# Own orders for the first two periods and the seventh period of a four-stage pipeline on one Trainium2 core

## The chip, the cores and the metric

The kernel runs on 1 core of one Trainium2 chip. The metric is device time in microseconds (us) of one execution. Three runs of the kernel before gave 4455.59, 4456.53 and 4457.14 us; the median is 4456.53 us.

## The reference

The input is `x`, four sequences of 2048 rows of 256 channels (float32). Four blocks follow each other, each wrapped as `x = x + layernorm(block(layernorm(x)))`:

```python
x = x + LN(softmax_attention(LN(x)))      # 16 heads of 16, q and k are scaled copies of the input, v is the input
x = x + LN(channel_mix(LN(x)))            # xk, xr: mixes of a row with the row before it; r = sigmoid(xr Wr)
                                          # out = r * (relu(xk Wk)^2 Wv)
x = x + LN(linear_attention_layer(LN(x))) # own LN, q/k through elu+1, message = Q (K^T V) / normaliser, residual,
                                          # own LN, gelu MLP 256 -> 1024 -> 256, residual
x = x + LN(gated_mlp(LN(x)))              # weights int32 / 127; silu(gate) * up, 256 -> 768 -> 256
```

The linear attention sums `K^T V` over all 2048 rows of a sequence, so the message of any row can only be made once the whole sequence has passed its keys and values.

## The kernel before, in words

The softmax attention comes first and is not touched. The rest of the reference is in `rest`. It cuts the 4 x 2048 rows into 16 blocks of 512 rows (`IB`, 4 blocks per sequence, `NBLK`), and gives each block four stages, written as Python generators that stop at named parts:

- `stage_f` is the channel mix. Parts: `sums` (statistics of the layernorm, on VectorE), `norm` (on ScalarE, after a power on GpSimd), `turn` (TensorE transposes into `hT`, ScalarE copies, and two VectorE copies that carry the last column to the next block), `mix` (ScalarE `shift`, VectorE `xk` and `xr`), `k0`, `k1`, `r`, `v` (matmuls), `osums`, `x` (output norm, residual on GpSimd, and a DMA that writes the block to the DRAM tile `mid`). Block 0 has no `sums` and `norm`: its `h0` is made ahead.
- `stage_a` is the first half of the linear attention: `sums`, `norm`, `norm2`, `turn`, `q0`, `q1` (into `QT`, through `elu1`), `kv0` to `kv4` (keys and values, gathered into one PSUM accumulator).
- `stage_b` is its second half: `pre`, `msg`, `sums`, `norm`, `turn`, `up0` to `up3`, `down0` to `down3`, `osums`, `x`.
- `stage_i` is the gated MLP: `sums`, `norm`, `turn`, `gate0` to `gate5`, `down0` to `down3`, `osums`, `x`.

A loop runs over 24 periods `p`. In period `p`, stage f is at block `p`, stage a at block `p-2` (`LAG_A`), stage b at block `p-6` (`LAG_B`), stage i at block `p-7` (`LAG_I`). So periods 0 and 1 hold stage f alone, periods 2 to 5 hold f and a, period 6 is the first with stage b, period 7 the first with stage i. `next:` and `last:` in an order name a part of the period after or before; parts of blocks outside 0 to 15 are skipped.

The order of the parts within a period is a written string: `RAMP` for periods 0 to 5, `FULL` for 6 to 17, `TURN` for 18, `LATE` after that. The instructions of TensorE (PE), ScalarE (ACT) and VectorE (DVE) go through `InOrder`, which keeps them in the program's order; they all carry line 46 in the profile. GpSimd (POOL) instructions and the DMAs issued by SyncE (SP) are placed by the scheduler. An engine works its own list strictly in order.

Resources that tie the parts: the pool `ps_m` has 5 PSUM tiles, taken in turn by every `mm_tile()`; `ps_t` has 2; the tag `tmp` (`shift`, `elu`, `gs`) has 3; `xk` and `r` share one buffer; `hT` has one. `convert` turns the int32 weights of the gated MLP into `wgT`, `wuT`, `wdT`: a DMA into a staging tile `wi`, then one DVE instruction. All three stagings use the one buffer of the tag `gT`. Before, `convert` runs at the start of periods 0, 1 and 2.

Of the kernel before, what the change touches and what calls it, by code (L numbers as in the profile page):

```python
# [49 lines left out]
def rest(ctx: ExitStack, tc: tile.TileContext, a: dict, out_rows, mids, env: dict, narrow: bool):  # L50
# [17 lines left out]
    NB = B * NBLK  # L68
    LAG_A, LAG_B, LAG_I = 2, 2 + NBLK, 3 + NBLK
# [11 lines left out]
    def convert(name):  # L81
        wi = one.tile(list(wq[name].shape), I32, tag="gT", name="wi")
        nc.sync.dma_start(out=wi, in_=a[name].rearrange("(c p) d -> p c d", p=P))
        dve.tensor_scalar(wq[name], wi, 1.0 if narrow else DEQUANT, None, ALU.mult)

    kvms, vs = [], []
    for r in range(3):
# [5 lines left out]
        v = one.tile([P, CC, P + 4], FP, tag=f"v{r}", name=f"v{r}")  # L93
# [57 lines left out]
    def load(j, pool):  # L151
        xs[j] = pool.tile([P, 4, C], FP, tag="x", name="x")
        nc.sync.dma_start(out=xs[j], in_=mids[j // NBLK][j % NBLK])
# [192 lines left out]
    def stage_i(j):  # L346
# [67 lines left out]
    FULL = (  # L414
        "f:turn i:turn b:msg i:gate0 a:turn f:mix last:i.osums i:gate1 b:sums last:i.x load i:gate2 "
        "i:gate3 f:k0 b:norm f:k1 f:r b:turn i:gate4 b:up0 i:gate5 f:v b:up1 f:osums b:up2 f:x b:up3 "
        "a:q0 next:f.sums b:down0 a:q1 next:a.sums b:down1 next:f.norm b:down2 next:a.norm b:down3 "
        "a:kv0 next:b.pre i:down0 b:osums a:kv1 i:down1 b:x a:kv2 next:a.norm2 i:down2 next:i.sums "
        "a:kv3 i:down3 a:kv4 next:i.norm"
    )  # L420
    RAMP = (
        "load f:turn a:turn f:mix a:q0 a:q1 f:k0 f:k1 next:a.sums a:kv0 a:kv1 next:a.norm a:kv2 "
        "next:f.sums a:kv3 f:r next:a.norm2 a:kv4 f:v next:f.norm f:osums f:x next:b.pre"
    )

    TURN = (
        "i:turn b:msg i:gate0 last:i.osums b:sums i:gate1 last:i.x load b:norm i:gate2 "
        "b:turn b:up0 next:b.pre b:up1 b:up2 b:up3 b:down0 b:down1 b:down2 b:down3 b:osums i:gate3 "
        "i:gate4 b:x i:gate5 next:b.msg i:down0 next:i.sums next:b.sums i:down1 "
        "next:i.norm i:down2 next:b.norm i:down3 next:i.turn"  # L430
    )
    LATE = (
        "last:i.osums b:turn b:up0 last:i.x load b:up1 b:up2 next:b.pre b:up3 b:down0 b:down1 b:down2 "
        "b:down3 b:osums i:gate0 i:gate1 b:x i:gate2 i:gate3 i:gate4 next:b.msg i:gate5 next:i.sums "
        "i:down0 next:b.sums i:down1 next:i.norm i:down2 next:b.norm i:down3 next:i.turn"
    )
    MAKE = {"f": (stage_f, 0), "a": (stage_a, LAG_A), "b": (stage_b, LAG_B), "i": (stage_i, LAG_I)}
    live = {}

    def step(p, stage, part):  # L440
        make, lag = MAKE[stage]
        j = p - lag
        if not 0 <= j < NB:
            return
        if (stage, j) not in live:
            live[stage, j] = make(j)
        name = next(live[stage, j])
        assert name == part, (stage, j, name, part)

    xs[0] = env["x0"]  # L450
    for p in range(NB + LAG_I + 1):
        if p < 3:
            convert(("wgT", "wuT", "wdT")[p])
        order = LATE if p > NB + LAG_A else TURN if p == NB + LAG_A else FULL if p >= LAG_B else RAMP
        for item in order.split():
            if item == "load":
                if p + 1 < NB:
                    load(p + 1, early)
                if 0 <= p + 1 - LAG_B < NB:
                    load(p + 1 - LAG_B, late)  # L460
                continue
            stage, part = item.split(":")
            at = p
            if stage in ("next", "last"):
                at = p + 1 if stage == "next" else p - 1
                stage, part = part.split(".")
            step(at, stage, part)
# [3 lines left out]
def sandwich_kernel(ctx: ExitStack, tc: tile.TileContext, a: dict, out: bass.AP):  # L471
# [490 lines left out]
    with tc.If(narrow == 1) as branch:  # L962
        rest(tc, a, out_rows, mids, env, True)
    with branch.Else():
        rest(tc, a, out_rows, mids, env, False)
# [54 lines left out]
```

## Time and profile before

| what | value |
|---|---|
| median of 3 runs | 4456.53 us |
| the profiled execution | 4454.68 us |
| its span, first to last instruction | 4452.8 us |
| PE busy over the span | 4186.2 us, 94% |
| DVE busy | 3380.2 us, 76% |
| ACT busy | 2853.3 us, 64% |
| POOL busy | 1098.8 us, 25% |
| mean granted PE clock | 0.98 |

`rest` begins at about 3030 us of the span. The busy times by period, with the boundaries put near the first `xk` matmul of a period (period 7 and 8: near the first gate matmul):

| stretch (us) | period | length | PE busy | DVE busy | ACT busy | POOL busy | PE clock |
|---|---|---|---|---|---|---|---|
| 3030 to 3064 | 0 | 34.00 | 16.73 | 17.70 | 14.65 | 11.12 | 0.70 |
| 3064 to 3091 | 1 | 27.00 | 20.84 | 17.48 | 13.00 | 15.89 | 0.84 |
| 3091 to 3125 | 2 | 34.00 | 28.62 | 21.51 | 19.95 | 15.23 | 0.95 |
| 3125 to 3159 | 3 | 34.00 | 28.71 | 22.02 | 20.53 | 10.42 | 0.95 |
| 3159 to 3193 | 4 | 34.00 | 28.51 | 21.50 | 19.76 | 10.43 | 0.95 |
| 3193 to 3229 | 5 | 36.00 | 26.44 | 25.84 | 20.52 | 12.70 | 0.91 |
| 3229 to 3299 | 6 | 70.00 | 61.34 | 35.11 | 29.32 | 26.48 | 0.90 |
| 3299 to 3377 | 7 | 78.00 | 73.82 | 37.98 | 46.28 | 30.32 | 1.00 |
| 3377 to 3459 | 8 | 82.00 | 75.88 | 42.63 | 46.28 | 39.54 | 0.98 |

How to read it: an average over the span says little here, as nearly 3030 us of it are the softmax attention. The change touches only periods 0, 1, 2 (its start) and 6. There no engine is full, so what counts is which engine waits for which, in order of time. Lines of the timeline give a start, a duration, the engine, the source line, the operation with `out<-in` by tile name, and in brackets the idle time before it and what ended that. A PE matmul on float32 shows as two instructions of the program's one.

### The profile page before, as it was taken

How to read it: one execution, taken by the hardware profiler on the slowest of the kernel's cores; microseconds unless marked ns; L12 is line 12 of the kernel's file. 1: busy time of each engine (PE TensorE's matmuls, PEld its weight loads, DVE VectorE, ACT ScalarE, POOL GpSimd, SP SyncE). 2: the span in 40 equal slices, each digit the busy share in tenths (PEclk: the TensorE clock that was granted, in tenths of full speed). 3: DMA queues.
4: the chain of work that ended last, by engine and by line, in shares of the span. 5: the costliest groups of instructions: out<-in, count | busy, mean ns of one | idle time of the engine just before them, and what ended most of it. 6: DMA issues, size and time to landing. Idle time of an engine off the chain costs nothing.

```text
span 4452.8 us, 69661 instructions
## 1 busy us (share of the span) xinstructions
PE 4186.2 (94%) x26369; PEld 2199.2 (49%) x26369; DVE 3380.2 (76%) x6734; ACT 2853.3 (64%) x3550; POOL 1098.8 (25%) x1655
## 2 busy tenths in 40 slices
PE   6999999999999999999999999986889899998998
PEld 3444444444444444444444444433456666666666
DVE  7888999988889998889998888865645545545333
ACT  2777777777777777777777777764555555554333
POOL 3011012310101321111131010003344444544344
PEclk9999999999999999999999999998999999999998
DMA  3001001110010110101011000002100000000000
GB/s 110 24 26 30 20 20 36 52 29 20 21 38 11 39 48 25 34 12 28 25 39 41 17 23 23 17 25 74 38 14 25 22 31 24 29 20 10 20 20 16
DMA packets 84570, 130.60 MB, mean 29 GB/s; under 512 B 21376, under 2 KB 41984, under 8 KB 84224
## 3 DMA queue, kind: packets, MB, share of 16 engines
q1 hardware_dynamic: 79184, 123.28, 9.2%
q8 instruction: 210, 3.44, 0.3%
q10 hardware_dynamic: 5040, 2.77, 0.2%
q14 instruction: 136, 1.11, 0.1%
HBM read 33.70 MB, written 25.17 MB: 13 GB/s over the span
## 4 chain that ended last, share of the span: by engine, by line
PE 72%; DVE 14%; ACT 8%; issue 3%; POOL 2%; DMA 1%; SPq 0%; ACTq 0%; DVEq 0%; POOLq 0%
PE acc L46 21%; PE s L46 19%; PE w L46 15%; PE m L46 14%; DVE mx L46 6%; PE t L46 2%; ACT h L46 1%; ACT p L46 1%; ACT L46 1%; DVE o L46 1%; DVE gs L46 1%; DVE lno_st L46 1%; ACT gs L46 1%; PE ot L46 1%; ACT zT L46 1%
## 5 line engine op out<-in xcount | busy, mean ns | idle before, releaser
L46 DVE TENSOR_REDUCE mx<-s 128x1 f32<-128x512 f32 x4096 | 2538.9, 683 | 249.8 <-PE s L46 249.6
L46 ACT ACTIVATE p<-w 128x1024 f32<-128x1024 f32 x2048 | 1995.7, 1022 | 808.6 <-PE s L46 515.5
L46 PE MATMUL s<-k,q 64*128 64x512 f32 x4096 | 1665.1, 450 | 29.9 <-DMA q<-lo 16.9
L46 PE MATMUL w<-mrow,pick 64*128 64x512 f32 x4096 | 1398.3, 417 | 0.0
L46 PE MATMUL w<-q,k 64*128 64x512 f32 x4096 | 1369.8, 419 | 0.0
L46 PEld LDWEIGHTS s<-k,q 64*128 64x128 f32 x4096 | 758.2, 186 | 1233.8 <-DVE mx L46 1123.2
L46 PE MATMUL acc<-p,xp 128*32 128x512 f32 x8192 | 1092.5, 605 | 0.0
L46 PEld LDWEIGHTS w<-mrow,pick 64*128 64x128 f32 x4096 | 748.8, 185 | 55.7
L46 PEld LDWEIGHTS w<-q,k 64*128 64x128 f32 x4096 | 669.9, 185 | 57.9 <-ACT p L46 21.0
L745 POOL TENSOR_SCALAR xm<-nm 128x16 fp32r<-128x16 f32 x64 | 17.6, 274 | 1565.9 <-DVE nm L46 1546.1
L46 PEld LDWEIGHTS acc<-p,xp 128*32 128x32 f32 x8192 | 161.6, 108 | 247.9 <-issue 246.7
L46 PE MATMUL m<-zT,w1T 128*128 128x512 f32 x512 | 229.5, 603 | 5.9 <-ACT zT L46 5.9
L46 PE MATMUL m<-w2T,hf 128*128 128x256 f32 x1024 | 225.6, 379 | 0.0
L46 PEld LDWEIGHTS m<-w2T,hf 128*128 128x128 f32 x1024 | 194.6, 190 | 38.4 <-issue 13.4
L46 DVE SCALAR_TENSOR_TENSOR gs<-m,gs 128x512 f32<-128x512 f32 x96 | 66.2, 690 | 193.5 <-ACT gs L46 159.1
L46 ACT ACT_TABLE_LOAD x94 | 120.6, 1283 | 117.2 <-PE m L46 83.2
L626 POOL TENSOR_SCALAR xp<-x,lnx_nm,lnx_rs 128x64 f32<-128x64 f32 x256 | 99.1, 394 | 374.5 <-PE acc L46 373.6
L644 POOL TENSOR_SCALAR xd<-x,lnx_nm,lnx_rs 128x128 f32<-128x128 f32 x256 | 110.8, 447 | 292.6 <-PE t L46 285.2
L46 ACT ACTIVATE elu<-elu 128x256 f32<-128x256 f32 (+1 forms) x96 | 46.8, 488 | 182.1 <-DVE elu L46 177.1
L46 PEld LDWEIGHTS m<-zT,w1T 128*128 128x128 f32 x512 | 97.5, 193 | 123.6 <-issue 98.4
L46 ACT ACTIVATE hf<-m,b 128x512 f32<-128x512 f32 x128 | 86.6, 686 | 99.3 <-PE m L46 98.8
L46 ACT CAST gT<-gs 128x512 fp32r<-128x512 f32 x96 | 59.4, 619 | 138.5 <-DVE gs L46 138.5
(160 smaller groups left out, 4265.0 us busy)
## 6 DMA issues: line engine op xcount, KB each, us to landing
q<-hi SPq DMA_DIRECT2D x256, 64.0 KB, 2.1
q<-lo SPq DMA_DIRECT2D x256, 64.0 KB, 2.1
mid<-x SPq DMA_DIRECT2D x31, 512.0 KB, 2.6
x<-mid SPq DMA_DIRECT2D x31, 512.0 KB, 3.3
k<-hi SPq DMA_DIRECT2D x240, 64.0 KB, 2.1
k<-lo SPq DMA_DIRECT2D x240, 64.0 KB, 2.1
x<-in_x SPq DMA_DIRECT2D x16, 512.0 KB, 5.6
out<-x SPq DMA_DIRECT2D x16, 512.0 KB, 2.8
```

Source lines behind the costliest of these rows:

```text
L46: return lambda *args, **kw: self._tc.keep_in_program_order(method(*args, **kw))
L626: nc.gpsimd.tensor_scalar(heads(n)[:, i, :, :HD], xs[b][:, i, g * GH * HD : (g + 1) * GH * HD].rearrange("p (h d) -> p h d", d=HD), nm[:, ...
L644: nc.gpsimd.tensor_scalar(xd[:, i], xh.unsqueeze(1).broadcast_to([P, 2, GH * HD]), nm[:, it : it + 1], rs[:, it : it + 1], ALU.add, ALU.mult,)
L745: nc.gpsimd.tensor_scalar(parts[..., 0], nm, 1.0, None, ALU.mult)
```

## The change

Three things are done to the order; no instruction of the arithmetic is added or taken away.

1. Periods 0 and 1 get orders of their own (`ALONE`). In period 0, the next block's `turn` stands ahead of this block's `v`, and the next block's `mix` ahead of this block's `osums` and `x`. In period 1, all of the next blocks' sums and norms are placed between the matmul parts, and `turn` and `mix` of its own block are gone, as they were done in period 0.
2. `convert` of `wgT` and `wuT` moves from the start of periods 0 and 1 into these orders: after `mix` in period 0, to the very end in period 1. `wdT` stays at the start of period 2.
3. Period 6 gets an order of its own (`FIRST`) in place of `FULL`: `mix` stands ahead of stage b's `msg`; `q0` and `q1` directly behind `msg`, ahead of `k0` and of stage b's `sums`; all of `up` and `down` follow each other, with `v` behind `down3`; `osums` and `x` of stage f go to the end of the period, `i.sums` behind `kv3`.

```diff
+    ALONE = (
+        "load f:turn f:mix convert next:f.sums f:k0 f:k1 next:f.norm f:r next:f.turn f:v next:f.mix "
+        "f:osums f:x",
+        "load f:k0 next:f.sums f:k1 next:a.sums f:r next:f.norm next:a.norm f:v next:a.norm2 f:osums "
+        "f:x convert",
+    )
+
+    FIRST = (
+        "f:turn a:turn f:mix b:msg a:q0 a:q1 f:k0 b:sums f:k1 load b:norm f:r b:turn b:up0 b:up1 b:up2 "
+        "b:up3 next:f.sums b:down0 b:down1 next:f.norm b:down2 next:a.sums b:down3 f:v next:a.norm "
+        "b:osums a:kv0 next:b.pre a:kv1 b:x a:kv2 next:a.norm2 a:kv3 next:i.sums f:osums a:kv4 "
+        "next:i.norm f:x"
+    )
...
     for p in range(NB + LAG_I + 1):
-        if p < 3:
-            convert(("wgT", "wuT", "wdT")[p])
-        order = LATE if p > NB + LAG_A else TURN if p == NB + LAG_A else FULL if p >= LAG_B else RAMP
+        if p == 2:
+            convert("wdT")
+        order = (
+            ALONE[p] if p < LAG_A else RAMP if p < LAG_B else FIRST if p == LAG_B
+            else FULL if p < NB + LAG_A else TURN if p == NB + LAG_A else LATE
+        )
         for item in order.split():
             if item == "load":
...
+                continue
+            if item == "convert":
+                convert(("wgT", "wuT")[p])
                 continue
```

In the built program this shows as follows. DVE's list has the conversion of `wuT` directly in front of that of `wdT`. SP's list has the DMA of `wdT` behind block 1's write to `mid`. ACT's list has two more activation table loads in period 6: before, that period loaded gelu's table, then the exponential's (ahead of `q0`); now it loads the exponential's (ahead of `q0`), the sigmoid's (ahead of `r`), gelu's, and the exponential's again (ahead of `kv0`).

## The prediction

> **What bounds the kernel now.** I read the page's chain first, then the chain in order of time around 3030 to 3300 us, then the timeline there.
>
> ```profile
> PE 72%; DVE 14%; ACT 8%; issue 3%; POOL 2%; DMA 1%; SPq 0%; ACTq 0%; DVEq 0%; POOLq 0%
> ```
>
> Over the span PE carries the end. In the periods that change it does not. The chain in order of time (start, us, what), at the ends of periods 0 and 1:
>
> ```profile
> 3056.63 1.04 POOL lno_rs L550
> 3057.70 2.19 DVE o L46 x4
> 3059.89 1.40 DVE wuT L46
> 3061.98 0.73 ACT shift L46
> ...
> 3085.14 2.20 DVE o L46 x4
> 3087.34 1.40 DVE wdT L46
> 3089.44 0.73 ACT shift L46
> ```
>
> Each period begins with `hT`'s carried column on DVE, and before that stand DVE's output norm and a weight conversion. The conversion itself found its data there long before, as the queue of SP shows (start, duration, queue, line):
>
> ```profile
> 3061.89 0.32 SPq L214 DMA_DIRECT2D mid<-hf  x1
> 3062.31 0.38 SPq L83 DMA_DIRECT2D wi<-in_wdT  x1
> ```
>
> The DMA of `wdT` went out at 3062.31, once `wuT`'s conversion (3059.81 plus 1.47) had freed the buffer, and landed 5.2 us later (the three DMAs of `wi` took 4.4, 4.5 and 5.2); it was used at 3087.27. Now period 6, timeline:
>
> ```profile
> 3228.72 1.88 DVE L46 SCALAR_TENSOR_TENSOR xk<-hT,mu_k,shift 128x512 f32<-128x512 f32 x2
> 3229.52 5.38 PE L46 MATMUL m<-xk,WkT 128*128 128x512 f32 x8 [5.51 <-DVE xk L46]
> 3236.68 2.08 ACT L46 ACTIVATE h<-hb,nb,lnb_rs 128x256 f32<-128x256 f32 x4 [2.87 <-POOL nb L119]
> 3241.04 3.70 PE L46 MATMUL m<-zT,w1T 128*128 128x512 f32 x8 [1.46 <-ACT zT L46]
> 3275.57 5.31 PE L46 MATMUL m<-wkv,zT 128*128 128x512 f32 x12
> 3283.90 2.20 DVE L46 TENSOR_SCALAR o<-o,lno_mv,lno_rs 128x256 f32<-128x256 f32 x4 [1.40 <-POOL lno_rs L550]
> 3291.48 2.08 ACT L46 ACTIVATE h<-x,nb,lni_rs 128x256 f32<-128x256 f32 x4
> ```
>
> PE waits for DVE's `xk`, then is solid from 3241.04 to 3283, and then waits while DVE and ACT finish b's output norm and `i.norm`; the first gate matmul of period 7 is at 3298.64. So the period's end is DVE's tail behind `down3`.
>
> **Periods 0 and 1.** I walk the engines' new lists with the old durations; times are on the old clock.
>
> *Period 0.* Up to `xr` (DVE free at 3042.84) nothing moves: the conversion of `wgT` at 3035.34 lay beside ACT's `h0` (to 3037.53) and cost nothing. It is now behind `xr`: 0.96, then block 1's sums 2.42, to 3046.2. POOL now squares both `ka` first (the second ready at 3047.41), then the power, 1.04, and `nb`: 3050.05. ACT's four `h`, 2.06, to 3052.1; the sigmoid load, 1.28; four `r`, 1.4, to 3054.8 (before: 3050.64). The transposes lie beside this. `v` needs the PSUM tiles that `r` frees, so it ends at 3056.5; ACT's copies of `hT` end at 3055.9; DVE's four `o` at 3057.45. Then `xk`: 3057.45 against 3062.74, **5.3 us earlier**. That is the gain of turning ahead.
>
> *Period 1.* DVE from there: `xk` and `xr` 2.75 (3060.2), osums 2.45, 1.2 for POOL's power, apply 2.2 (3066.05), sums of block 2 2.4, sums of `a` 2.45 (3070.9). POOL's power and `nb` 1.75, ACT's `h`, and DVE's sums for the second norm end at 3075.75; `o` 1.4, osums 2.45, power 1.3, apply 80.9 to 83.1. Here `hT`'s column could be copied at 3083 instead of 3088.66. But DVE has `wuT` in front (1.47, to 3084.5), and behind it `wdT`, whose DMA now needs that same buffer. On SP it also stands behind the write of `mid`, which waits for POOL's residual (first apply plus 0.5, plus 3.68): 3085.1. With the old pair's spacing (0.42) and its landing of 5.2, `wdT` lands at 3090.7. Conversion 0.96 (1.47 only beside POOL), the column copies 0.35: ACT's `shift` starts at 3092.15 against 3089.44. **Sum: +2.7 us**, where 5.3 had been won. Behind the waiting conversion on DVE stand the column copies, `xk`, `xr` and the whole of period 2; the matmuls `q0` and `q1` go ahead, but nothing else.
>
> Bounds: +1.3, if the DMA lands in 4.4 and the walk is 0.6 too late; +4.2, if the first matmuls of period 1 run at half speed, as before (6.44 for eight against 3.70), which puts POOL's power 1.0 later. I take the middle because the same pair of DMAs stood in the same order before. The move of `wdT`'s cover is the cost: hidden, it would be -4.2.
>
> In period 2 PE idles about 5 us ahead of `k0`. In the row of period 6 above eight matmuls took 5.38 after 5.51 idle; the old period 2 had 3.70 after 2.68. So 1.7 us are lost there, but DVE reached `kv0` at 3100.55 with the keys done at 3096.3: hidden. Periods 2 to 5 keep their lists and lengths, as DVE's first instruction sets them.
>
> **Period 6**, without that shift. `xk` goes from 3228.72 to 3226.4, so `k0` no longer waits. But:
>
> - `msg` on DVE starts at 3229.2 instead of 3225.51 (four times 0.82, to 3232.5). `q0` takes the fifth PSUM tile, `q1` needs the first `msg` tile: PE idles 3.8 us.
> - `elu` of `q0`, `q1` now stands ahead of b's sums on DVE: 0.69, then 2.04 waiting for ACT (table load 1.28, exponential 0.63), 0.69, then 0.69, 0.76, 0.69: 5.5 us, to 3238.0. Before, these waits lay in DVE's idle time under `up` and `down`. Sums 2.45, power and `nb` 1.75: ACT's `h` at 3242.2 instead of 3236.68.
> - Behind it comes the sigmoid load, 1.28, ahead of `r` and `zT`: first `up` at 3247.6 instead of 3241.04, 6.55 later.
> - PE then has less to do up to `down3`: `v` (3.45) and both `q` (3.44) are out of it. `down3` ends at 3275.3 against 3275.57. So far **-0.3**.
> - The tail on DVE, from the `o` of `down3` at 3275.5: `o` of `v` to 3279.4 (before, under `up`); second-norm sums 2.45 (before, ahead of `down3`); b's osums 2.5; `kv0` 2.65 with the exponential's load of 1.28 inside; `kv1` 1.35; apply 2.15; `kv2` 1.4; `kv3` 3.2, as ACT's four `h` of `norm2` (2.07) stand in front of its exponential; `i.sums` 2.5. Sum 22.1, to 3297.6; before, 13.95 from 3275.78 to 3289.73. **+7.9**.
> - POOL and ACT follow as before: `i.norm` at 3299.3 instead of 3291.48. DVE's osums and apply of stage f (2.45, 1.3, 2.2) run beside it, to 3303.4, ahead of `hT`'s column and `hL`. First gate matmul between 6.7 and 7.85 later: I take **+7.1**.
>
> Bounds of period 6: +4.6 if the load and ACT's `h` lie beside the wait for POOL; +8.5 if the cold PE adds a microsecond in its transposes. Period 7 is PE's: it idles 1.22, 0.48 and 0.35 us there in its first 30 us for ACT, and from period 8 on blocks leave every 82.05 us. Nothing gives the shift back.
>
> **Sum.** +2.7 + 7.1 = +9.8 us on the profiled 4454.68: 4464.5. The median of the runs is 1.85 above it: **4466.3**, say 4466. With the bounds +5.9 to +12.7: 4462.4 to 4469.2. A measurement of this kernel tells about 0.2%, 8.9 us, from no change, so the forecast lies on the edge of "slower".
>
> The Trainium skill, "ScalarE: Activation LUTs", section "What ACT_TABLE_LOAD costs", puts a switch of tables at 1283 ns for the load plus about 1380 ns of drain. The trace agrees on the load (1.28) but not on a drain in the chain: at 3093.62 a load starts, and its activation starts at 3094.91. By the page, an estimate: the three loads that now stand in the chain would add 3 x 1.38 = 4.1 us, to some 4470; I go by the row.
>
> **The rivals.**
>
> - *The order does what it says (faster).* If `wdT`'s DMA were out before `wuT`'s conversion, or DVE's wait for it lay beside others, periods 0 and 1 would give -4.2; if besides the first gate matmul followed `down3` (-0.3) and not DVE's tail, period 6 would give -0.3. 4452. It decides by one point: whether `shift` of period 2 starts before 3089.4. Against it: one buffer for three stagings, and DVE's lists. Chance 0.08.
> - *One loss only.* Period 1's cover holds (-4.2 + 7.1, 4459.4), or period 6's tail is absorbed because `kv` and the norms overlap better than I string them (+2.7, 4459.2). For it: a walk by hand tends to add waits that overlap. Chance 0.24.
> - *Dearer.* Cold PE in periods 1, 6 and 7 and POOL's powers queued behind `hb` (4.84 us for four) add 4 to 6: 4471. Chance 0.08.
> - *The forecast*: 0.60.
>
> **How the numbers follow.** The forecast's own range is 4462.4 to 4469.2. To leave out no more than 2 in 10, the range takes in the single losses and part of the dear case: 4458 to 4470.5. Slower by over 0.2% means over 4465.4: two thirds of the forecast's chance and the dear case, 0.49. Faster by over 0.2% is below 4447.6, further than the faster rival: 0.05. Within: 0.46.
>
> **What would show it.** DMA of `wdT` issued after the conversion of `wuT`, with DVE idle 5 to 6 us ahead of its conversion "<-DMA wi"; period 1's `xk` some 5 us earlier; period 2's `shift` near 3092; a PE wait for a PSUM tile ahead of `q1`; first `up` 6 to 7 us later on the period's own clock, `down3` level; `kv0` with a table load. Wrong would be a `shift` of period 2 before 3089.4, or DVE's tail behind `down3` under 18 us.

## The result, and the profile after

| | kernel before | changed kernel |
|---|---|---|
| median | 4456.45 us (8 runs, 4455.56 to 4457.54) | 4469.83 us (8 runs, 4465.73 to 4471.16) |
| profiled execution | 4454.68 us | 4465.73 us |
| its span | 4452.8 us | 4463.9 us |
| ratio | | 1.003, 95% interval 1.002 to 1.0039 |

The change makes the kernel 13.4 us (0.3%) slower. The profiled execution of the changed kernel is the fastest of its eight, so the pair of profiles differs by 11.05 us only.

The chain on the profile's page hardly shows it: PE 71% where it was 72%. The chain in order of time shows the loss of the first two periods at the end of period 1 (start, us, what):

```profile
3071.33 3.30 DMA x<-mid
3074.73 2.25 POOL hb L574 x2
...
3076.97 0.18 issue
3077.15 1.22 POOL hb L574
3078.37 1.00 POOL lnz_rs L570
3079.38 1.22 POOL hb L574
...
3081.09 1.01 POOL lno_rs L570
...
3082.62 3.71 POOL x L141 x4
...
3086.35 0.32 SPq L214
...
3086.76 5.03 DMA wi<-in_wdT
...
3091.81 0.96 DVE wdT L46
...
3092.94 0.73 ACT shift L46
```

Where DVE's `o`, a conversion and `shift` followed each other, there is now POOL's residual, SP's write of `mid`, and the DMA of `wdT` behind it. `shift` of period 2 stands at 3092.94 against 3089.44. Of these 3.50 us, 0.86 are not the change's: the stretch ahead of `rest`, the same in both kernels, ended that much later (first `shift` at 3040.28 against 3039.42). In period 1, `xk` came 4.46 us earlier on the raw clock, 5.32 on its own.

The timeline of period 6:

```profile
3230.22 1.42 DVE L46 SCALAR_TENSOR_TENSOR xk<-hT,mu_k,shift 128x512 f32<-128x512 f32 x2 [0.78 <-ACT shift L46]
3233.87 3.63 PE L46 MATMUL m<-zT,wqT 128*128 128x512 f32 x4 [3.81 <-DVE zr L46]
3238.81 0.69 DVE L46 SCALAR_TENSOR_TENSOR QT<-m,elu 128x512 f32<-128x512 f32 x1 [2.04 <-ACT elu L46]
3245.61 2.07 ACT L46 ACTIVATE h<-hb,nb,lnb_rs 128x256 f32<-128x256 f32 x4 [3.82 <-POOL nb L119]
3250.92 15.67 PE L46 MATMUL m<-zT,w1T 128*128 128x512 f32 x32 [1.85 <-ACT zT L46]
3280.44 0.42 DVE L46 TENSOR_TENSOR o<-m,b 128x256 f32<-128x256 f32 x1 [0.69 <-PE m L46]
3291.20 0.42 DVE L46 SCALAR_TENSOR_TENSOR K<-m,elu 128x256 f32<-128x256 f32 x1 [1.82 <-ACT elu L46]
3299.11 0.42 DVE L46 SCALAR_TENSOR_TENSOR K<-m,elu 128x256 f32<-128x256 f32 x1 [2.44 <-ACT elu L46]
3303.61 2.07 ACT L46 ACTIVATE h<-x,nb,lni_rs 128x256 f32<-128x256 f32 x4 [3.60 <-POOL nb L119]
```

Before, eight of the `up` matmuls stood at 3241.04 (3.70 us), the other 24 here:

```profile
3248.03 10.46 PE L46 MATMUL m<-zT,w1T 128*128 128x512 f32 x24
```

In brackets stands the idle time before an instruction and what ended it. PE waits 3.81 us for `msg` ahead of `q1`; the 32 matmuls of `up` start at 3250.92; DVE waits 2.04 us inside `elu` of `q0`, 1.82 inside `kv0` (with a table load), 2.44 inside `kv3` (behind the `h` of `norm2`). From the `o` of `down3` (3280.44) DVE needs 21.26 us to the start of the last instruction of `i.sums` (0.17 long, at 3301.70); before, 13.78 (3275.78 to 3289.56). `i.norm` starts at 3303.61 against 3291.48.

For the experiments I cut each profile at the same four points and take differences against the profile of before, in us. "Period 2" is the `xk` of period 2, counted from the first `shift` of period 0. "Period 6" is `i.norm`, counted from the copy of `hT`'s column at the period's start. "Tail" is DVE's time from the start of `down3`'s `o` to that of the last instruction of `i.sums` (the time itself, not a difference). "Time" is the median against the median of before on the same chip.

| kernel | period 2 | period 6 | tail | time |
|---|---|---|---|---|
| before | 0 | 0 | 13.78 | 0 |
| changed | +2.64 | +8.30 | 21.26 | +13.4 |
| again | +3.02 | +8.24 | 21.26 | +12.3 |
| alone | +3.12 | +0.17 | 13.82 | +2.4 |
| first | +0.35 | +8.06 | 21.25 | +6.4 |
| first_again | +0.64 | +8.14 | 21.26 | +10.2 |
| cover | -3.58 | -0.02 | 13.79 | -2.6 |
| tail | +0.52 | +2.74 | 19.91 | +3.7 |
| head | -1.61 | +4.44 | 13.59 | +3.2 |
| norm2 | +0.59 | +6.21 | 19.35 | +6.5 |
| b6 | +0.44 | +0.25 | 12.83 | +0.1 |
| b8 | -0.98 | -2.98 | 9.51 | +14.1 |
| best | -4.58 | -2.99 | 9.52 | +13.8 |
| best2 | -3.93 | -2.99 | 9.52 | -6.7 |

### The profile page after: what moved, and what is told of

It is laid out like the page before. It is cut to its first block, busy times and chain, and to the rows that moved or that the text cites. A ratio compares the mean times of both kernels' runs of the same rounds, so it can differ in the third digit from the quotient of the medians.

```text
span 4463.9 us, 69660 instructions
## 1 busy us (share of the span) xinstructions
PE 4186.0 (94%) x26369; PEld 2197.8 (49%) x26369; DVE 3378.8 (76%) x6734; ACT 2855.7 (64%) x3552; POOL 1097.6 (25%) x1655
## 4 chain that ended last, share of the span: by engine, by line
PE 71%; DVE 14%; ACT 8%; issue 3%; POOL 2%; DMA 1%; SPq 0%; ACTq 0%; DVEq 0%; POOLq 0%
PE acc L46 21%; PE s L46 19%; PE w L46 15%; PE m L46 14%; DVE mx L46 6%; PE t L46 2%; ACT h L46 2%; ACT p L46 1%; ACT L46 1%; DVE lno_st L46 1%; DVE o L46 1%; DVE gs L46 1%; ACT gs L46 1%; ACT elu L46 1%; PE ot L46 1%
```

## The experiments

**The changed kernel again, and its two halves.** No edit; then only one half of the change:

```diff
 # alone
-            ALONE[p] if p < LAG_A else RAMP if p < LAG_B else FIRST if p == LAG_B
+            ALONE[p] if p < LAG_A else RAMP if p < LAG_B
 # first: ALONE gone in place of FIRST, and convert at the start of periods 0, 1, 2 as before
-            ALONE[p] if p < LAG_A else RAMP if p < LAG_B else FIRST if p == LAG_B
+            RAMP if p < LAG_B else FIRST if p == LAG_B
```

> The changed kernel once more, for its spread: its eight first runs lay between 4465.73 and 4471.16 us, those of the kernel before between 4455.56 and 4457.54. Theory A (the two losses have one size each, and the fastest run is the rule): 9 to 12 us above the kernel before, as in the profiled pair (+11.05). Theory B (one of the new waits has no fixed length, so that the time itself is scattered): the median again 12 to 15 us above, with runs at least 3 us apart, and a profiled execution that is longer than the first one where one of the waits of period 1, 2 or 6 is longer.

> The new orders in periods 0 and 1 alone; period 6 has its old order. My theory (wdT's DMA waits for wuT's conversion, and the carried column of period 2 for wdT's): 2.5 to 3.5 us slower than the kernel before, shift of period 2 some 2.7 us later, xk of period 1 some 5 us earlier. Rival 1 (the order does what it says): 4 us faster. Rival 2 (all of the loss comes from period 6): 0. If the scatter of the changed kernel comes from the waits for DMAs in periods 1 and 2, it shows here.

> The new order of period 6 alone; periods 0 and 1 have their old order. My theory (first up 6.5 us later, PE level again at down3, then DVE's tail of 21 to 22 us instead of 14): 7 to 8 us slower than the kernel before; first gate matmul of period 7 some 7.5 us later. Rival 1 (the tail is absorbed in period 7): 0 to 1. Rival 2 (the cold PE adds to it): 9 to 11. If the scatter of the changed kernel comes from PE's clock in period 6, it shows here and not with the first two periods alone.

(In the ratios, the 95% interval stands in brackets.) Again: 4468.48 us (4467.15 to 4470.04), ratio 1.0027 (1.0017 to 1.0038). Alone: 4458.55 us, ratio 1.0005 (0.9996 to 1.0014), so +2.4 us, which the interval alone would not tell from nothing; the trace has it, `xk` of period 1 is 4.98 us earlier on its own clock and that of period 2 3.12 us later. First: 4462.53 us, ratio 1.0017 (1.0008 to 1.0026); its eleven runs stand in two groups, seven from 4461.58 to 4464.03 at a mean granted PE clock of 0.981 and four from 4466.52 to 4467.46 at 0.979. Both halves lose, as I had said, and each in its own place; the rival that the order does what it says falls for both.

For the scatter, again's profiled execution took 4470.04 us, 4.31 more than the changed kernel's first one. By the same cuts, 0.70 of that lie ahead of `rest`, 0.38 in periods 0 and 1, nothing in periods 2 to 6 up to `i.norm` (-0.05), 1.19 between `i.norm` and the first gate matmul, and 2.08 behind that, down to the last output. The fourth part is seen line by line in PE's timeline, first the changed kernel, then again:

```profile
3306.21 1.97 PE L46 MATMUL t<-ident,h 128*128 128x128 f32 x8 [4.55 <-ACT hT L46]
3307.97 2.44 PE L46 MATMUL m<-kvm,QT 128*128 128x132 f32 x16
3310.16 0.48 PE L46 MATMUL m<-hT,wgT 128*128 128x512 f32 x1
```

```profile
3307.24 1.97 PE L46 MATMUL t<-ident,h 128*128 128x128 f32 x8 [4.55 <-ACT hT L46]
3309.00 3.73 PE L46 MATMUL m<-kvm,QT 128*128 128x132 f32 x16
3312.38 0.78 PE L46 MATMUL m<-hT,wgT 128*128 128x512 f32 x1
```

After the same idle time of 4.55 us, the same sixteen matmuls take 2.44 us in one execution and 3.73 in the other; the granted clock over 7.5 us from the first transpose on is 0.82 and 0.60. The Trainium skill, "TensorE: Matmul & The Clock Gate", section "What's actually happening", says that the gate watches a free-running window of about 3.4 us, so that the number of cold matmuls (those at the low clock) varies from run to run; the two rows agree with that. So theory B holds in part: the waits themselves kept their length, and the 1.19 us come from PE's clock and not from a DMA. Of the 2.08 behind, 0.44 lie ahead of the output of block 0, again at a lower clock (0.98 and 0.96), and 1.51 between the outputs of blocks 7 and 12, where the granted clocks of the two executions hardly differ (0.99 and 1.00, then 0.95, 0.93, 0.88 and 0.94 in both); what makes these longer stays open.

**Is it the cover of wdT's DMA?**

```diff
 # alone, and in ALONE[1]:
-        "load f:k0 next:f.sums f:k1 next:a.sums f:r next:f.norm next:a.norm f:v next:a.norm2 f:osums "
-        "f:x convert",
+        "load f:k0 next:f.sums f:k1 next:a.sums convert f:r next:f.norm next:a.norm f:v next:a.norm2 f:osums "
+        "f:x",
```

> As the new orders in periods 0 and 1 alone, with one thing moved: wuT's conversion stands in period 1 behind a.sums of the next blocks, where DVE waits for ScalarE anyway, so that wdT's DMA goes out some 10 us earlier. My theory (the wait for this DMA is what turns the gain of the first two periods into a loss): 3 to 4.5 us faster than the kernel before, 6 to 7 us faster than with wuT's conversion at the end, no wait for wi at wdT's conversion. Rival (the wait moves to another place: residual, reload or the norms of the next blocks): not faster than the kernel before.

4453.59 us, ratio 0.9994 (0.9985 to 1.0003): 5.0 us below alone, 2.6 below before. By the medians that is less than I had expected (6 to 7, and 3 to 4.5), and the interval against before takes in 1; the traces carry the argument. DVE's timeline, first alone, then cover:

```profile
3085.58 1.48 DVE L46 TENSOR_SCALAR wuT<-wi 128x1536 fp32r<-128x1536 int32 x1
3093.33 0.96 DVE L46 TENSOR_SCALAR wdT<-wi 128x1536 fp32r<-128x1536 int32 x1 [6.27 <-DMA wi<-in_wdT]
```

```profile
3071.63 0.95 DVE L46 TENSOR_SCALAR wuT<-wi 128x1536 fp32r<-128x1536 int32 x1
3084.11 1.48 DVE L46 TENSOR_SCALAR wdT<-wi 128x1536 fp32r<-128x1536 int32 x1
```

The DMA goes out at 3072.61 instead of 3088.08, the wait of 6.27 us is gone, and `xk` of period 2 moves from +3.12 to -3.58: 6.70 us by one moved word. The gain of turning ahead was there all the time and was lost to this wait. The median tells 5.0 of the 6.7.

**Which half of FIRST?** Head and tail of the new order apart, and one wait of the tail alone, all with the old orders in periods 0 and 1:

```diff
 # tail: FULL's head, FIRST's tail
+        "f:turn b:msg a:turn f:mix b:sums load f:k0 b:norm f:k1 f:r b:turn b:up0 b:up1 b:up2 b:up3 a:q0 ... a:q1 ..."
 # head: FIRST's head, FULL's tail
+        "f:turn a:turn f:mix b:msg a:q0 a:q1 f:k0 b:sums ... b:up0 f:v b:up1 f:osums b:up2 f:x b:up3 ..."
 # norm2: FIRST, but
-        "... next:a.norm2 a:kv3 next:i.sums ..."
+        "... a:kv3 next:a.norm2 next:i.sums ..."
```

> Period 6 with the old head (msg ahead of mix, q0 and q1 among up and down) and only the new tail (v behind down3, osums and x of stage f at the end, i.sums behind kv3); periods 0 and 1 as before. My theory (the loss is DVE's list behind down3, which is longer by v's four o, the sums moved behind it and the exponential that waits for norm2): down3 ends some 3.45 us earlier, as v is no longer in front of it, DVE's tail is 20 us instead of 14 (no table load in kv0, as q0 has loaded the exponential's table), i.norm 2.7 us later, and the time 1.5 to 3.5 us above the kernel before. Rival (the head is the whole loss): 0 or faster.

> Period 6 with only the new head (mix ahead of msg, q0 and q1 directly behind msg), and v, osums and x of stage f back among up; the tail as before; periods 0 and 1 as before. My theory (the head puts the first up 6 us later, and with v among up again PE can't make that good; q0 and q1 leave the stretch, 3.4 us): down3 4.3 us later, one more table load of 1.28 ahead of kv0, i.norm 4.3 to 5.6 us later, the time 3.5 to 6 us above the kernel before. Rival (turning ahead pays, and the tail is the whole loss): 0 or faster. The two halves of the order together should come to the 8.1 us that i.norm was later with the whole new order of period 6.

> The new order of period 6 alone, with next:a.norm2 moved behind kv3, so that ScalarE makes kv3's exponential ahead of the four h of the second norm (2.06 us). My theory (this wait stands in DVE's list ahead of i.sums): i.norm 2.0 us earlier than with the new order of period 6 as it is, that is 6 us later than in the kernel before, and the time 4 to 5 us above it. Rival (DVE's next wait takes its place): i.norm as late as with the new order, 8 us.

Tail: 4459.50 us, ratio 1.0007 (0.9998 to 1.0016). Head: 4459.01 us, the same ratio and interval. Norm2: 4462.26 us, ratio 1.0013 (1.0004 to 1.0022). The traces settle it better than the times: period 6 is 2.74 longer with the tail alone (2.7 expected), 4.44 with the head alone (4.3 to 5.6 expected), together 7.2 of the whole order's 8.06; the other 0.9 is not traced. `down3`'s `o` comes 3.39 us earlier in the one and 4.63 later in the other, counted from the period's start. The times are +3.7 and +3.2, each just outside what I had expected (1.5 to 3.5, 3.5 to 6); head's periods 0 and 1, the old ones, happened to be 1.6 us short in its profile. Norm2 shortens period 6 by 1.85 of the expected 2.0 and DVE's tail from 21.25 to 19.35; in the medians this can't be seen (+6.5, where I had expected 4 to 5), as that of first itself moved (next).

> The new order of period 6 alone, the same kernel once more: its eleven runs stood in two groups, 4461.6 to 4464.0 (seven) and 4466.5 to 4467.5 (four), and the profiled one was of the upper group. Theory A (TensorE's clock: in the lower group period 6 or the last periods run with fewer cold matmuls): the profiled execution, if it is of the lower group, shows i.norm still 8 us later by its own clock and loses its microseconds elsewhere, in the wait for the first gate matmul or behind 3900 us. Theory B (the walk is wrong in the lower group): i.norm only 3 to 4 us later. If it is of the upper group again, the question stays open.

4466.33 us, ratio 1.0022 (1.0013 to 1.0031), on the same edit that gave 4462.53. Its profile has period 6 at +8.14 and the first gate matmul at 0.78 us, cold, as in first's. It was of the upper group once more (4467.37), so there is no trace of a lower run. The record has one hint: in both runs of this kernel the clock goes with the time, 0.981 in the lower group and in first_again's fastest run (4463.41), 0.978 or 0.979 in all others. So the groups go with PE's clock; in which periods, no trace shows, and the runs of the changed kernel and of the kernel before aren't sorted by it. Both medians together bracket my +7.1.

**Another order for period 6.** Statistics and norms drawn into DVE's idle time under `up` and `down`:

```diff
 # b6, in place of FIRST (periods 0 and 1 as before)
+        "f:turn b:msg a:turn f:mix b:sums load f:k0 b:norm f:k1 f:r b:turn b:up0 f:v b:up1 "
+        "f:osums b:up2 f:x next:f.sums next:a.sums b:up3 a:q0 b:down0 a:q1 next:f.norm "
+        "next:a.norm b:down1 b:down2 next:a.norm2 b:down3 b:osums a:kv0 next:b.pre b:x a:kv1 "
+        "next:i.sums a:kv2 a:kv3 a:kv4 next:i.norm"
```

> Another order for period 6: head and tail as in the kernel before, but the next blocks' sums and norms drawn into VectorE's idle time under up and down, and kv0 behind b.osums, so that less stands behind down3; periods 0 and 1 as before. Theory (DVE's list behind down3 sets the end of the period): i.norm 1 to 2.5 us earlier than in the kernel before, the time 1 to 2.5 us below it. Rival (the output norm's power on GpSimd waits behind the four hb of norm2, 4.84 us, so that the next wait takes over): 0, or slower by up to 1.5.

4455.94 us, ratio 1.0 (0.9991 to 1.0009): the rival. POOL's timeline names the wait that took over (DVE's apply idles 3.23 us for this power); below it the same place with `hb` held in the program's order (b8):

```profile
3278.95 0.72 POOL L337 TENSOR_TENSOR o<-o,hb 128x256 f32<-128x256 f32 x1 [1.44 <-DVE o L46]
3279.78 4.85 POOL L574 TENSOR_SCALAR hb<-x,lna_mv,lna_rs 128x256 f32<-128x256 f32 x4
3284.60 1.04 POOL L570 TENSOR_TENSOR lno_rs<-lno_ve,neghalf 128x4 f32<-128x4 f32 x1
```

```profile
3277.25 0.72 POOL L337 TENSOR_TENSOR o<-o,hb 128x256 f32<-128x256 f32 x1 [1.44 <-DVE o L46]
3279.59 1.04 POOL L46 TENSOR_TENSOR lno_rs<-lno_ve,neghalf 128x4 f32<-128x4 f32 x1 [1.61 <-DVE lno_ve L46]
```

The scheduler starts `hb` of a block two periods ahead as soon as its buffer is free, here when the residual of the last `down` (`o<-o,hb`) has read it, and puts 4.85 us in front of the power that the period waits for. The kernel before had it in the same place (`hb` at 3278.02, the power at 3282.83, and DVE's apply idle for 1.40 us).

```diff
 # b8: b6, and in rest
-    pe, act, dve = (InOrder(tc, e) for e in (nc.tensor, nc.scalar, nc.vector))
+    pe, act, dve, pool = (InOrder(tc, e) for e in (nc.tensor, nc.scalar, nc.vector, nc.gpsimd))
-            ln_apply(hb[:, i, :], x[:, i, :], mv, rs, i, nc.gpsimd)
+            ln_apply(hb[:, i, :], x[:, i, :], mv, rs, i, pool)
     # the powers of rest's sums on pool too; next:b.pre first in RAMP, behind b:up1 in period 6
 # best: b8, cover, and wdT's convert between f:osums and f:x of period 1
 # best2: best, and in FULL
-        "... b:turn i:gate4 ... a:kv0 next:b.pre i:down0 ..."
+        "... b:turn next:b.pre i:gate4 ... a:kv0 i:down0 ..."
```

> As the other order for period 6 (sums and norms drawn into VectorE's idle time), and the four hb of the next blocks held in the program's order on GpSimd, as the powers are: hb of stage b's first block at the start of period 5, of its second behind up1 in period 6, instead of as soon as their buffers come free. Periods 0 and 1 as before. Theory (hb, 4.85 us in front of the output norm's power, is what kept the drawn-in order from gaining: 3284.60 instead of 3281.2): i.norm 2.5 to 3.2 us earlier than in the kernel before, the time 2 to 3 us below it. Rival (the next wait, ScalarE's or the residual's, takes over): 0 to 1 us below.

> All that the runs point to: the new orders of periods 0 and 1 with wuT's conversion behind a.sums and wdT's conversion between osums and x of period 1 (VectorE waits 1.16 us for GpSimd there), hb held in the program's order, and the other order for period 6. Theory: shift of period 2 some 4.5 to 5 us earlier than before, i.norm of period 6 another 2.5 to 3 us earlier: 6 to 8 us below the kernel before. Rival (with wdT gone the next wait of period 2 is zT on ScalarE, and the gains of period 6 don't add): 3 to 5 us below.

> As the kernel with all that the runs point to, but with hb's place in FULL moved from behind kv0 to behind b's turn, where GpSimd made it in the kernel before; the first seven periods are unchanged. Theory (held in the program's order, hb stood in front of b's output norm in every period from the eighth on, and that cost the 17 us behind the first gate matmul): the first gate matmul again 6.9 us earlier than before, the rest as long as before, the time 5.5 to 7.5 us below the kernel before. Rival (the order of the powers or the shorter first periods themselves cost it): again 8 us or more above.

B8: 4470.23 us, ratio 1.0031 (1.0019 to 1.0044). Best: 4469.97 us, ratio 1.0029 (1.0019 to 1.004). In both the first seven periods did as the theory said (period 6 -2.98 and -2.99; best's first gate matmul 6.92 us earlier than before), and the rest lost some 17 us in best's profile and 19 in b8's. The place: in best, outputs of the blocks 0 to 7 leave 83.56 us apart ((3975.71 - 3390.82) / 7), where it was 82.05. POOL in period 8, first best, then best2:

```profile
3436.04 4.85 POOL L46 TENSOR_SCALAR hb<-x,lna_mv,lna_rs 128x256 f32<-128x256 f32 x4
3440.86 1.04 POOL L46 TENSOR_TENSOR lno_rs<-lno_ve,neghalf 128x4 f32<-128x4 f32 x1
```

```profile
3434.90 0.74 POOL L337 TENSOR_TENSOR o<-o,hb 128x256 f32<-128x256 f32 x1
3439.00 1.04 POOL L46 TENSOR_TENSOR lno_rs<-lno_ve,neghalf 128x4 f32<-128x4 f32 x1 [3.36 <-DVE lno_ve L46]
```

I had held `hb` to where `FULL` names it, in front of the output norm, in every period; the scheduler had made it earlier. Best2 moves that one word: 4449.27 us (4447.24 to 4450.68) against 4456.00, ratio 0.9984 (0.9975 to 0.9993), the blocks 82.06 us apart. It beats the kernel before by 6.7 us and the changed one by some 20.

## Why the prediction was right or wrong, point by point

Both losses are where the prediction put them, and alone, first, cover, tail, head and norm2 take them apart. The sum was 3.5 us too low: 4469.83 lies above the forecast's own range (to 4469.2), and inside the stated one (to 4470.5) only by the part of the dear case that it took in.

- *Period 0, `xk` 5.3 us earlier.* Right: 5.32 on its own clock.
- *Period 1, the wait for `wdT`: +2.7.* Right in the mechanism and its size: the DMA went out behind `wuT`'s conversion and the write of `mid`, landed 5.03 us later (5.2 taken), DVE idled 6.07 us ahead of the conversion, sum +2.64. Cover shows that it is this wait: -3.58 without it, where I had put -4.2. The seven profiles with the old order in periods 0 and 1 and the old place of `hb` scatter from -1.61 to +0.64 themselves (I did not trace why), so the loss is 2.6 give or take one. The upper bound of +4.2 does not follow from the 1.0 us named with it (2.7 + 1.0 = 3.7); the case did not come, as the first eight matmuls of period 1 took 3.70.
- *What I missed there.* POOL's `hb` for block 0 sits ahead of the powers of period 1 and waited 0.91 us for block 0's reload (`x<-mid`), both in the chain shown above. I had named POOL's queue of `hb` under "Dearer" only. The first `o` of the apply started at 3082.13, 0.38 later than my 80.9 shifted by the late start (81.75). The sum came out all the same, by chance: the shorter landing and shorter copies took the 0.38 back.
- *Periods 2 to 5 keep their lengths.* Off by +0.33, and by 0.33 to 0.35 in the other profiles with the new first periods and the old place of `hb`, against 0.03 to 0.08 with the old ones; I did not trace why.
- *Period 6, head: "-0.3 at down3".* The term that was mis-sized: +0.83, as `down3`'s `o` came at 51.76 us from the period's start against 50.93. First `up` was 6.05 us later (6.55 taken). But from there to this `o` PE took 29.52 us against 34.74, 5.2 less, where leaving out `v` and both `q` was to save 6.9. The 32 matmuls of `up` were cold: 15.51 us (to the first `down` at 3266.43) against 13.83, with a granted clock of 0.51 in the first 3.5 us, where it had been 1.00. Again, first and first_again show the same row at 15.60, 15.44 and 15.53. `q1` was cold too (3.63 us for four where `q0` took 1.88), but it stands ahead of the first `up` and did not delay it.
- *Period 6, tail: 22.1 us.* 21.43, counted to the end of `i.sums` as the prediction did, against 13.95: +7.5. Both together make `i.norm` +8.30, where I had +7.8.
- *From `i.norm` to the end.* I took 0.7 off for the stretch to the first gate matmul, and nothing behind it. The profiled execution has 0.61 off there (+7.69 for the period); again's has 0.58 added, which is the "microsecond of cold PE" that I had as a bound (8.82 for the period, the bound was 8.5). The median of the changed kernel is close to again's profiled time (4470.04); no trace shows which kind its other runs are.
- *The sum.* +9.8 on the profiled 4454.68; +11.05 measured between profiles, +13.4 and +12.3 between medians. Of the 11.05, 0.86 lie ahead of `rest`. So 2.5 to 3.6 us are missing in the median: about 0.5 in `i.norm` (the cold `up`, 1.7, less what other terms came short of) and 0.3 in periods 2 to 5. The rest I can't place for the median; in again's profile it lies behind `i.norm`, 1.2 up to the first gate matmul from PE's clock and 2.1 behind it, mostly without a cause shown. How often each kernel meets the cold case I can't tell from the runs.
- *The rule on table loads.* The three loads that now stand in the chain show no drain. The loads at 3236.85 and 3247.70 (1.28 each) are followed by their activations at 3238.14 and 3248.99. Behind the load at 3289.46 (1.28 long) the exponential of `kv0` and its `K` at 3291.20 follow: 0.42 for the exponential leaves 0.04 us. The row decided rightly against the 4.1 us estimated from the skill's page. That these would have led to some 4470, next to the median, is chance: what was missing was not in the loads.
- *The rivals.* "The order does what it says" would have needed cover's edit. "One loss only" falls: alone and first each lose. "Dearer", at 4471, lies within 1.2 us of the median; it named the cold PE, which is the cause of the part of the excess that could be traced, and POOL's `hb`, whose 0.38 us in period 1 were made up.

## What to carry to other kernels

A weight conversion that is pushed behind other work takes the next conversion's DMA with it, through the staging buffer and the in-order queue; ask where the next transfer into the same buffer will be issued before moving the instruction that frees it. What is moved out of an idle stretch of an engine (here statistics and `o` out of DVE's idle time under `up` and `down`) comes back at full price at the period's end. And a scheduler that starts work greedily can be right in the steady state and wrong in the ramp: hold the order only where the trace shows that it hurts, then look at what the hold does to all other periods.

## What the runs showed of the hardware that I had not expected

The same sixteen matmuls, after the same 4.55 us of idle time and the same eight transposes, took 2.44 or 3.73 us, at granted clocks of 0.82 and 0.60, in two executions of one program. The times of first scatter by 6.4 us (4461.58 to 4467.99 over both runs of it), in groups that go with the granted clock, where the kernel before scatters by about 3.6 (4454.41 to 4458.01 in 30). A weight conversion on DVE took 0.95 us or 1.48, the longer in every profile where POOL's residual ran beside it, as for `wdT` in the rows of cover; beside one of POOL's powers (`wuT` there) it took 0.95, and the power 1.67 instead of 1.04.
